# Four heads per update of x, context read back by batch, and the inner layer of batches 1 to 3 turned to [feature, token], in a two-block gated transformer kernel

## The chip, the cores and the metric

The kernel runs on one core of one Trainium2 chip. The metric is the device time of one execution in microseconds (us). The engines named below are PE (TensorE, matmuls), PEld (its weight loads), DVE (VectorE), ACT (ScalarE), POOL (GpSimd) and SP (the queue that issues most DMAs). PSUM is the memory that PE writes; it has eight banks here, each of 128 partitions x 512 float32.

## The reference

Four batches (b) of 512 tokens x 512 features pass through two blocks. Everything is float32 at the interface. Cut to what is computed:

```python
# block 0: adjacency from the context, top 153 of 512 per row, made symmetric
sim  = einsum(Q, K) / (sqrt(32) * 4);  keep = sim >= 153rd largest of its row
A    = sigmoid(sim) * keep;  A = (A + A.T) / 2
x    = x + tanh(g_x[0]) * ((1 - gamma) * layernorm(x) + gamma * A)
# block 0: feed-forward, Hadamard-rotated, 8-bit activations, ternary weights
h    = act_quant(fwht(layernorm(x)))          # fwht over 512
y    = silu(h @ gate.T) * (h @ up.T)          # 2048 features: the inner layer
x    = x + tanh(g_f[0]) * (act_quant(fwht(y)) @ down.T)   # fwht over 2048
# block 1: latent attention, 16 heads, keys and values from the context (kv, 128 wide, with rope)
q_r  = rope(layernorm(x) @ Wq @ w_kc_q) @ W_qr;  k_r = rope(kv) @ W_kr
x    = x + tanh(g_x[1]) * sum_h( softmax(q_r @ k_r.T) @ rope(kv) @ (w_kc_kv[h] @ Wo[h]) )
# block 1: feed-forward with rms norm, 8-bit activations, ternary weights
x    = x + tanh(g_f[1]) * (n + act_quant(silu(gate(n)) * value(n)) @ out.T)
```

## The kernel before

Each batch's 512 tokens are four tiles (j) of 128 tokens on the partitions, kept in SBUF as `xs[b, j]`. The program has three stages.

**Start.** Batch 0 goes alone through block 0 (`adjacency(0)`, `feed0(0, w0)`), while the weights of block 0's feed-forward are made ternary (`ternary`) and `ahead` prepares the attention: it multiplies the context by its rope tables on POOL (`kv[b]`, one tile for each batch that stays in SBUF for the whole kernel), and multiplies `w_kc_kv[h]` by `Wo[h]` into one 128 x 512 matrix for each head, which is stored to DRAM (`om_d[h]`).

**Attention with background work.** `attention` runs over 32 pairs of heads (4 batches x 8 pairs, class `Pair`). A pair has four steps j; each computes the scores of two heads, the softmax (DVE row maximum, ACT exp, DVE reciprocal, ACT scaling) and the transposes of the probabilities (`turn`); in between the next pair's queries are made (`head`, `rope`, `rotated`). Then `attended` multiplies by `kv` into `pc`, which ACT copies to `cxo`, and `added` multiplies by the two heads' `om` into PSUM (`po`, two products summed for each j) and DVE adds it to x (L870). The loads of `om` are issued by `out_weights` at the start of the pair.

Between the steps, generators of background work are advanced by estimated costs: `before(b)` (adjacency, keys and `feed0` of the next batch) during the attention of the batch before it, and `last_weights` (the ternary weights of block 1 and `feed1` of batches 0 to 2) during batch 3. In `feed0` of batches 1 to 3, `gated` multiplies the quantized tokens of a tile `zq` by the ternary weights `wa` (float8): for each of four groups o of 512 features, four matmuls make the gate in `pg`, four the up part in `pu`, with tokens on the partitions; ACT applies silu with the token's scale (L307), DVE multiplies (L308). `back` does the Hadamard transform over 2048 features: butterflies across the sixteen blocks of 128 features on DVE (L551), then, in four rounds, four PE transposes (`ph`, L557), a copy to SBUF on ACT (`yT`, L559), four matmuls with the 128 x 128 Hadamard matrix (`pzh`, L563) and a scaled copy on ACT (`yb`, L564). `projected` finds the row maximum, quantizes, transposes and multiplies by the down weights (`pd`, L399).

**End.** `feed1` of batch 3 and the rest of the background work.

A list scheduler orders every engine's instructions when the program is built, by priority (the order of the program, shifted in `high_priority` blocks) and by its own estimate of durations; on the chip each engine runs its list strictly in order. PSUM has four banks for the attention (`mm`), two for transposes (`tr`) and two for background work (`bg`): in the background `pg`, `pu`, `ph`, `pzh` and `pd` all take turns in the two `bg` banks. A float32 matmul is recorded as two PE records, a float32 transpose or a bfloat16 or float8 matmul as one.

Of the kernel before, what the change touches and what calls it, by code (L numbers as in the profile page):

```python
# [2 lines left out]

# [23 lines left out]
EPS = 1e-5  # L27
MAGIC = 12582912.0
GONE = -3.0e38
F8 = mybir.dt.float8e4  # L30


@with_exitstack
def flamingo_kernel(
# [51 lines left out]
    def front_t(name):  # L86
        if mine("front", 2):
            return two_k("front", 3, name)
        return wp.tile([P, 512], F32, tag="pp", name=name, bufs=7)

    def gate_t(name):
        if alone[0]:
# [122 lines left out]
    def ternary(specs, names, hold):  # L215


        found = []

        def piece(src, inner, i, name):  # L220
            t = big(f"{name}{i}")
            marks["load"] = nc.sync.dma_start(
                t if inner == 1 else t.rearrange("p (c o) -> p c o", c=inner), src(i)
            )
            return t

        for (src, inner, n, dst, count), name in zip(specs, names):
            acc = small.tile([P, n], F32, tag=f"wacc{n}", name=f"acc_{name}")
            held = []
            for i in range(n):  # L230
                t = piece(src, inner, i, f"sa_{name}")
                held.append(t)
                junk = bp.tile([P, FF], BF, tag="q", name=f"ja_{name}{i}") if hold else t
                nc.scalar.activation(junk, t, AF.Abs, accum_out=acc[:, i : i + 1])
                yield 4.0
            tot = small.tile([P, 1], F32, tag="wtot", name=f"tot_{name}")
            nc.vector.tensor_reduce(tot, acc, AX.X, ALU.add)
            pt = bg_ps(f"pt_{name}")
            marks["sum"] = nc.tensor.matmul(pt[:, 0:1], ones, tot, start=True, stop=True)
            sc = const.tile([P, 1], F32, tag=f"ws_{name}", name=f"ws_{name}")  # L240
            nc.vector.tensor_scalar(sc, pt[:, 0:1], 1.0 / count, EPS, ALU.mult, ALU.max)
            inv = const.tile([P, 1], F32, tag=f"wi_{name}", name=f"wi_{name}")
            nc.vector.reciprocal(inv, sc)
            found.append(sc)
            for i in range(n):
                t = held[i] if hold else piece(src, inner, i, f"sb_{name}")
                nc.scalar.activation(t, t, AF.Identity, scale=inv, bias=magic[:, 0:1])
                marks["sign"] = nc.scalar.activation(
                    dst(i), t, AF.Sign, bias=magic[:, 1:2], saturate=False
                )  # L250
                yield 4.0
        return found
# [42 lines left out]
    def gated(u, zq, wa, dg, y):  # L295

        for o in range(4):
# [10 lines left out]
            nc.vector.tensor_tensor(y[:, o * 512 : (o + 1) * 512], sg, pu, ALU.mult)  # L308
            yield 0.9

    reached = []

    def tiles(name, ready, wa, back, spread):
# [186 lines left out]
    def feed0(b, w):  # L500
# [44 lines left out]
        def back(j, ya, du):  # L545
            u = f"f{b}_{j}"
            yb = big(f"yb_{u}")

            for src, dst, g in ((ya, yb, 8), (yb, ya, 4), (ya, yb, 2), (yb, ya, 1)):
                for args in butterfly(src, dst, "p (g t q) -> p g t q", {"g": g}):  # L550
                    nc.vector.tensor_tensor(*args)  # L551
                    yield 1.3
            for k in range(4):
                pt = bg_tr(f"ph_{u}_{k}")
                for c in range(4):
                    at = (4 * k + c) * P
                    nc.tensor.transpose(pt[:, c, :], ya[:, at : at + P], ident)  # L557
                hT_ = back_t(f"yT_{u}_{k}")
                nc.scalar.copy(hT_, pt.rearrange("p c q -> p (c q)"))  # L559
                pz = bg_ps(f"pzh_{u}_{k}")  # L560
                for c in range(4):
                    cols = slice(c * P, (c + 1) * P)
                    nc.tensor.matmul(pz[:, cols], hT_[:, cols], had_sb, start=True, stop=True)  # L563
# [84 lines left out]

    NG = NH // 2
    kv, hT = {}, {}  # L650
    om_d, kr_d = {}, {}
    spilled = {}

    def ahead():
# [5 lines left out]
        sin_k = wp.tile([P, NT, DC], F32, tag="rs", name="sin_k", bufs=3)  # L660
        nc.gpsimd.dma_start(sin_k, sink)
        hf = DC // 2
        for b in range(B):
            cb = wp.tile([P, NT, DC], F32, tag="qh", name=f"cb_{b}")
            nc.gpsimd.dma_start(cb, cx[b * S : (b + 1) * S, :].rearrange("(j p) d -> p j d", p=P))
            t = const.tile([P, NT, DC], F32, tag=f"kv{b}", name=f"kv_{b}")
            nc.gpsimd.tensor_tensor(t, cb, cos_k, ALU.mult)
            rt = wp.tile([P, NT, DC], F32, tag="rs", name=f"rt_{b}", bufs=3)
            nc.gpsimd.tensor_tensor(rt[:, :, :hf], cb[:, :, hf:], sin_k[:, :, :hf], ALU.mult)
            nc.gpsimd.tensor_tensor(rt[:, :, hf:], cb[:, :, :hf], sin_k[:, :, hf:], ALU.mult)  # L670
            nc.gpsimd.tensor_tensor(t, t, rt, ALU.add)
            kv[b] = t
        yield
        for h in range(NH):
            wv = hp.tile([P, DC], F32, tag="wk", name=f"wv_{h}", bufs=3)
# [5 lines left out]
            om = wp.tile([P, D], F32, tag="cxo", name=f"oms_{h}", bufs=3)  # L681
# [6 lines left out]

    def keys(b):

        pt = bg_tr(f"pkv_{b}")
        for j in range(NT):
            nc.tensor.transpose(pt[:, j, :], kv[b][:, j, :], ident)
# [4 lines left out]
        for g in range(NG):  # L698
# [2 lines left out]
            pk = gate_ps(f"pk_{b}_{g}")  # L701
            nc.tensor.matmul(pk, wk, kvT, start=True, stop=True)
            if alone[0]:
                k = wp.tile([P, S], F32, tag="cxo", name=f"krs_{b}_{g}", bufs=3)
            else:
                k = front_t(f"krs_{b}_{g}")
            nc.scalar.copy(k, pk)
# [5 lines left out]
    def hidden_T(b):  # L713
        mv, r = ln_stats([xs[b, j] for j in range(NT)], f"q{b}")
        t = hp.tile([P, NC, S], F32, tag="hT", name=f"hT_{b}", bufs=1)
        for j in range(NT):
            n = wp.tile([P, D], F32, tag="pp", name=f"nq_{b}_{j}", bufs=7)
# [21 lines left out]
    def out_weights(b, g):  # L739

        oms = []
        for h in (2 * g, 2 * g + 1):
            om = hp.tile([P, D], F32, tag="om", name=f"om_{b}_{h}")
            nc.sync.dma_start(om, om_d[h])
            oms.append(om)
        return oms
# [7 lines left out]
    class Pair:  # L754
# [60 lines left out]
        def scores(self, j):  # L815
# [12 lines left out]
            for i in range(2):  # L828
                v = f"{self.u}_{i}_{j}"
                nm = small.tile([P, 1], F32, tag="nm", name=f"nm_{v}")  # L830
                nc.vector.tensor_reduce(nm, pss[i], AX.X, ALU.max, negate=True)  # L831
                pp = wp.tile([P, S], F32, tag="pp", name=f"pp_{v}", bufs=7)
# [15 lines left out]
        def attended(self):  # L848
            self.cxo = []
            for i in range(2):  # L850
                pc = mm_ps(f"pc_{self.u}_{i}")
                for l in range(NT):
# [4 lines left out]
                cxo = wp.tile([P, S], F32, tag="cxo", name=f"cxo_{self.u}_{i}", bufs=3)  # L857
                nc.scalar.copy(cxo, pc)  # L858
                self.cxo.append(cxo)

        def added(self):
            for j in range(NT):
                po = mm_ps(f"po_{self.u}_{j}")
                for i in range(2):
                    nc.tensor.matmul(  # L865
                        po, self.cxo[i][:, j * P : (j + 1) * P], self.oms[i],
                        start=(i == 0), stop=(i == 1),
                    )
                t = xs[self.b, j]
                nc.vector.scalar_tensor_tensor(t, po, tgx1, t, ALU.mult, ALU.add)  # L870
# [6 lines left out]
    def attention(first):  # L877
# [4 lines left out]
        for at, (b, g) in enumerate(order):  # L882
# [256 lines left out]
```

## Time and profile before

| | |
|---|---|
| median of 3 runs | 2063.09 us (2061.5 to 2064.79) |
| the profiled execution | 2064.35 us, span 2062.6 us |
| PE busy | 1853.7 us (90%), 7274 records |
| DVE busy | 1584.7 us (77%) |
| ACT busy | 1176.6 us (57%) |
| POOL busy | 333.1 us (16%) |
| DMA | 139.25 MB, mean 68 GB/s |
| mean granted TensorE clock | 0.962 |

The span divides into the start (to about 290 us), the attention with background work (to about 1970 us) and the end. Inside the attention, the gating of batches 1, 2 and 3 (L302) lies at 487 to 583, 904 to 1007 and 1321 to 1424 us, and block 1's weights are made ternary between 1451 and 1578 us. A busy PE is not PE at its peak, since the ends of matmul records are modelled; the distance from the start of one record to the start of the next is the better price of a matmul in a stream.

### The profile page before, as it was taken

The page shows a single profiled execution, that of the slowest core. Times are in us where ns is not written, and L with a number is a line of the kernel's source. Part 1 is how long each engine was busy: PE and PEld are TensorE (multiplying, and loading weights), DVE is VectorE, ACT ScalarE, POOL GpSimd, SP SyncE. Part 2 cuts the span into 40 slices and gives each one's busy share as a digit, 9 for nine tenths or more (in the row PEclk, how much of TensorE's full clock was granted, in tenths as well). Part 3 has the DMA queues.
Part 4 walks back from the last instruction along what each step waited for, and adds up shares of the span by engine and source line. Part 5 has one row for each costly group of instructions (what it writes and reads, how often), then busy time and mean ns, then how long its engine had stood idle before and what let it go on. Part 6 is the DMA issues. An engine that isn't in the chain of part 4 may idle for free. (4 is left out here: it accounts for less than half of the span.)

```text
span 2062.6 us, 21752 instructions
## 1 busy us (share of the span) xinstructions
PE 1853.7 (90%) x7274; PEld 873.3 (42%) x7274; DVE 1584.7 (77%) x3233; ACT 1176.6 (57%) x1979; POOL 333.1 (16%) x316
## 2 busy tenths in 40 slices
PE   1268789999999999999999999999999999999898
PEld 0035434434544444445453444454444444444344
DVE  7989599986774999876769999767636755866775
ACT  6935454455544555455454554554899565567554
POOL 3010031122100221230011221300112210101000
PEclk6579899999999999999999999999999999999999
DMA  7451021210101222110012221101755111111000
GB/s 273 148 177 38 1 77 41 63 46 27 38 21 32 83 82 60 43 38 26 27 33 87 72 73 38 38 21 33 256 191 199 50 38 45 58 35 39 11 16 26
DMA packets 65633, 139.25 MB, mean 68 GB/s; under 512 B 7537, under 2 KB 18161, under 8 KB 62449
## 3 DMA queue, kind: packets, MB, share of 16 engines
q1 hardware_dynamic: 60048, 121.92, 18.7%
q0 software_dynamic: 4320, 14.16, 1.8%
q10 hardware_dynamic: 1152, 1.77, 0.2%
q8 instruction: 58, 0.95, 0.2%
q14 instruction: 55, 0.44, 0.1%
HBM read 117.90 MB, written 19.92 MB: 67 GB/s over the span
## 5 line engine op out<-in xcount | busy, mean ns | idle before, releaser
L793 POOL TENSOR_TENSOR ro<-ro,rs 128x512 f32<-128x512 f32 x192 | 252.7, 1319 | 1167.2 <-DVE rs L789 753.8
L834 ACT ACTIVATE pp<-pss,nm 128x512 f32<-128x512 f32 x256 | 175.1, 688 | 224.8 <-DVE nm L831 224.0
L764 PE MATMUL pqh<-hT,wq 128*128 128x512 f32 x512 | 239.6, 603 | 6.8 <-ACT pp L834 6.6
L853 PE MATMUL pc<-pT,kv 128*128 128x512 f32 x512 | 235.4, 598 | 0.7 <-ACT pT L846 0.6
L865 PE MATMUL po<-om,cxo 128*128 128x512 f32 x512 | 230.9, 597 | 0.0
L831 DVE TENSOR_REDUCE nm<-pss 128x1 f32<-128x512 f32 x256 | 167.6, 681 | 57.4 <-PE pss L826 56.5
L779 PE MATMUL pb<-qh,wc 128*128 128x512 f32 x384 | 191.1, 614 | 10.4 <-ACT qh L769 7.3
L449 DVE MAX8 m<-work 128x8 f32<-128x512 f32 x304 | 198.0, 680 | 0.6
L454 DVE MATCH_REPLACE8 work<-m,work 128x512 f32<-128x512 f32 x288 | 192.8, 674 | 0.1
L837 ACT ACTIVATE pp<-pp,rsm 128x512 f32<-128x512 f32 x256 | 178.9, 724 | 21.2 <-DVE rsm L836 20.9
L870 DVE SCALAR_TENSOR_TENSOR x<-po,gt,x 128x512 f32<-128x512 f32 x128 | 94.6, 744 | 92.4 <-PE po L865 91.9
L846 ACT COPY pT<-ppt 128x512 f32<-128x512 f32 x256 | 142.9, 592 | 28.9 <-PE ppt L845 28.8
L845 PEld LDWEIGHTS ppt<-ident,pp 128*128 128x128 f32 x1024 | 117.3, 141 | 86.0 <-issue 33.9
L845 PE MATMUL ppt<-ident,pp 128*128 128x128 f32 x1024 | 146.4, 277 | 6.7 <-ACT pT L846 3.5
L823 PE MATMUL pss<-kr,qr 64*128 64x512 f32 x256 | 144.3, 644 | 5.6 <-ACT pp L834 4.8
L764 PEld LDWEIGHTS pqh<-hT,wq 128*128 128x128 f32 x512 | 92.7, 191 | 125.4 <-issue 84.6
L826 PE MATMUL pss<-kr,qr 64*128 64x512 f32 x256 | 144.4, 645 | 0.5 <-DVE ro L787 0.5
L865 PEld LDWEIGHTS po<-om,cxo 128*128 128x128 f32 x512 | 93.7, 190 | 114.5 <-issue 98.1
L787 DVE TENSOR_TENSOR ro<-pb,cos_q 128x512 f32<-128x512 f32 x192 | 130.5, 680 | 11.0 <-PE pb L779 10.2
L853 PEld LDWEIGHTS pc<-pT,kv 128*128 128x128 f32 x512 | 92.7, 190 | 102.3 <-issue 88.7
L858 ACT COPY cxo<-pc 128x512 f32<-128x512 f32 x64 | 37.6, 587 | 135.7 <-PE pc L853 135.4
L750 PE MATMUL pr<-ro,wr 128*64 128x512 f32 x192 | 99.8, 613 | 14.3 <-POOL ro L793 12.2
(266 smaller groups left out, 3123.5 us busy)
## 6 DMA issues: line engine op xcount, KB each, us to landing
wq<-in_wqh SPq DMA_DIRECT2D x64, 256.0 KB, 2.7
om<-omd SPq DMA_DIRECT2D x64, 256.0 KB, 2.7
wc<-in_wkcq SPq DMA_DIRECT2D x32, 384.0 KB, 3.1
krd<-krs POOLq DMA_DIRECT2D x32, 256.0 KB, 2.4
kr<-krd SPq DMA_DIRECT2D x32, 256.0 KB, 2.7
sa_w1v<-in_gvT SPq DMA_DIRECT2D x8, 1024.0 KB, 5.3
sb_w1v<-in_gvT SPq DMA_DIRECT2D x8, 1024.0 KB, 5.5
wr<-in_wqr SPq DMA_DIRECT2D x32, 192.0 KB, 2.4
```

The costliest lines, as they stand in the source:

```text
L449: nc.vector.max(m8[j], cur[j])
L454: nc.vector.match_replace(works[j], m8[j], cur[j], GONE)
L764: nc.tensor.matmul(pq, self.wqs[i][:, c, :], hT[self.b][:, c, :], start=(c == 0), stop=(c == NC - 1),)
L779: nc.tensor.matmul(pb, self.wc[:, at : at + P], self.qhs[i if i < 2 else o], start=True, stop=True)
L793: nc.gpsimd.tensor_tensor(ro, ro, rs, ALU.add)
L826: nc.tensor.matmul(*args, start=True, stop=True)
L831: nc.vector.tensor_reduce(nm, pss[i], AX.X, ALU.max, negate=True)
L834: nc.scalar.activation(pp, pss[i], AF.Exp, bias=nm, accum_out=sm)
L837: nc.scalar.activation(pp, pp, AF.Copy, scale=rs)
L845: nc.tensor.transpose(pt[:, l, :], pp[:, l * P : (l + 1) * P], ident)
L853: nc.tensor.matmul(pc, kv[self.b][:, l, :], self.pT[i][:, l, :], start=(l == 0), stop=(l == NT - 1),)
L865: nc.tensor.matmul(po, self.cxo[i][:, j * P : (j + 1) * P], self.oms[i], start=(i == 0), stop=(i == 1),)
```

## The change

**x updated for four heads at once.** `added` runs for every second pair only and takes the `cxo` and `om` of both pairs: four products are summed in PSUM for each j, and DVE adds the sum to x. `cxo` gets four buffers (from three), `om` four (from two); `pp`, the tile of probabilities, gets six (from seven).

**Context read back by batch.** `ahead` goes through the batches from 3 down to 0; the rope'd contexts of batches 3, 2 and 1 are stored to DRAM on POOL's queue, and `keys(b)` reads them back on SP's. `kv` now has two buffers in place of four tiles.

**Inner layer of batches 1 to 3 as [feature, token].** `gated_turned` takes the weights as the stationary operand and the tokens as the moving one, 128 columns at a time, so that y has features on the partitions, block by block. Each token's scale then lies along the free axis: it is spread over a 128 x 128 row tile (DVE, one PE product with the identity, ACT copy), DVE multiplies `pg` by it, and ACT applies silu in SBUF. The four transposes and the copy of each round in `back` are gone: `pzh` reads y.

**One step of the ternary weights of block 1 on DVE.** Where the weights are not held (`hold` false), the scaling with the rounding constant moves from ACT to DVE.

```diff
     def front_t(name):
-        return wp.tile([P, 512], F32, tag="pp", name=name, bufs=7)
+        return wp.tile([P, 512], F32, tag="pp", name=name, bufs=6)
...
                 t = held[i] if hold else piece(src, inner, i, f"sb_{name}")
-                nc.scalar.activation(t, t, AF.Identity, scale=inv, bias=magic[:, 0:1])
+                if not hold:
+                    nc.vector.tensor_scalar(t, t, inv, MAGIC, ALU.mult, ALU.add)
+                else:
+                    nc.scalar.activation(t, t, AF.Identity, scale=inv, bias=magic[:, 0:1])
...
+    def gated_turned(u, zq, wa, dg, y):
+        row = front_t(f"dgr_{u}")
+        nc.vector.tensor_scalar(row[:, :P], ones, dg, None, ALU.mult)
+        pt = bg_ps(f"pdg_{u}")
+        nc.tensor.matmul(pt[:, :P], row[:, :P], ident, start=True, stop=True)
+        nc.scalar.copy(row[:, P : 2 * P], pt[:, :P])
+        row = row[:, P : 2 * P].unsqueeze(1).to_broadcast([P, 4, P])
+        for o in range(4):
+            pg = gate_ps(f"pg_{u}_{o}")
+            pu = gate_ps(f"pu_{u}_{o}")
+            for pw, at in ((pg, FF + o * 512), (pu, o * 512)):
+                for f in range(4):
+                    cols = slice(at + f * P, at + (f + 1) * P)
+                    for c in range(NC):
+                        nc.tensor.matmul(
+                            pw[:, f * P : (f + 1) * P], wa[:, c, cols], zq[:, c, :],
+                            start=(c == 0), stop=(c == NC - 1),
+                        )
+            sg = gate_t(f"sg_{u}_{o}")
+            nc.vector.tensor_tensor(
+                sg.rearrange("p (f t) -> p f t", f=4), pg.rearrange("p (f t) -> p f t", f=4), row, ALU.mult
+            )
+            nc.scalar.activation(sg, sg, AF.Silu)
+            nc.vector.tensor_tensor(y[:, o * 512 : (o + 1) * 512], sg, pu, ALU.mult)
+            yield 0.9
...
-            return gated(f"{name}_{j}", zq, wa, dg, y), back(j, y, du)
+            made = gated_turned if spread and not alone[0] else gated
+            return made(f"{name}_{j}", zq, wa, dg, y), back(j, y, du)
...
-                pt = bg_tr(f"ph_{u}_{k}")
-                for c in range(4):
-                    at = (4 * k + c) * P
-                    nc.tensor.transpose(pt[:, c, :], ya[:, at : at + P], ident)
-                hT_ = back_t(f"yT_{u}_{k}")
-                nc.scalar.copy(hT_, pt.rearrange("p c q -> p (c q)"))
+                if quick:
...
+                else:
+                    hT_ = ya[:, 4 * k * P : 4 * (k + 1) * P]
...
-        for b in range(B):
+        for b in reversed(range(B)):
...
-            kv[b] = t
+            if b == 0:
+                kv[b] = t
+            else:
+                kv_d[b] = dram.tile([P, NT, DC], F32, tag=f"kvd{b}", name=f"kvd_{b}")
+                nc.gpsimd.dma_start(kv_d[b], t)
...
     def keys(b):
+        if b:
+            kv[b] = wp.tile([P, NT, DC], F32, tag="kv", name=f"kvr_{b}")
+            nc.sync.dma_start(kv[b], kv_d[b])
...
-        def added(self):
+        def added(self, before):
+            cxo, oms = before.cxo + self.cxo, before.oms + self.oms
             for j in range(NT):
                 po = mm_ps(f"po_{self.u}_{j}")
-                for i in range(2):
+                for i in range(4):
                     nc.tensor.matmul(
-                        po, self.cxo[i][:, j * P : (j + 1) * P], self.oms[i],
-                        start=(i == 0), stop=(i == 1),
+                        po, cxo[i][:, j * P : (j + 1) * P], oms[i], start=(i == 0), stop=(i == 3)
                     )
...
-            cur.added()
+            if g % 2:
+                cur.added(last)
+            last = cur
```

More of the change, by code (lines that the diff above doesn't have):

```diff
@@ L1 @@
 import math
-from contextlib import ExitStack
+from contextlib import ExitStack, nullcontext
 import concourse.bass as bass
@@ L29 @@
 GONE = -3.0e38
+U16 = mybir.dt.uint16
 F8 = mybir.dt.float8e4
@@ L553, in back @@
             for k in range(4):
-                pt = bg_tr(f"ph_{u}_{k}")
-                for c in range(4):
-                    at = (4 * k + c) * P
-                    nc.tensor.transpose(pt[:, c, :], ya[:, at : at + P], ident)
-                hT_ = back_t(f"yT_{u}_{k}")
-                nc.scalar.copy(hT_, pt.rearrange("p c q -> p (c q)"))
+                if quick:
+                    pt = bg_tr(f"ph_{u}_{k}")
+                    for c in range(4):
+                        at = (4 * k + c) * P
+                        nc.tensor.transpose(pt[:, c, :], ya[:, at : at + P], ident)
+                    hT_ = back_t(f"yT_{u}_{k}")
+                    nc.scalar.copy(hT_, pt.rearrange("p c q -> p (c q)"))
+                else:
+                    hT_ = ya[:, 4 * k * P : 4 * (k + 1) * P]
                 pz = bg_ps(f"pzh_{u}_{k}")
@@ L650, in flamingo_kernel @@
     kv, hT = {}, {}
-    om_d, kr_d = {}, {}
+    om_d, kr_d, kv_d = {}, {}, {}
     spilled = {}
@@ L662, in ahead @@
         hf = DC // 2
-        for b in range(B):
+        for b in reversed(range(B)):
             cb = wp.tile([P, NT, DC], F32, tag="qh", name=f"cb_{b}")
             nc.gpsimd.dma_start(cb, cx[b * S : (b + 1) * S, :].rearrange("(j p) d -> p j d", p=P))
-            t = const.tile([P, NT, DC], F32, tag=f"kv{b}", name=f"kv_{b}")
+            t = wp.tile([P, NT, DC], F32, tag="kv", name=f"kv_{b}")
             nc.gpsimd.tensor_tensor(t, cb, cos_k, ALU.mult)
@@ L680, in ahead @@
             nc.tensor.matmul(po, wv, wo, start=True, stop=True)
-            om = wp.tile([P, D], F32, tag="cxo", name=f"oms_{h}", bufs=3)
+            om = wp.tile([P, D], F32, tag="cxo", name=f"oms_{h}", bufs=4)
             nc.scalar.copy(om, po)
@@ L703, in keys @@
             if alone[0]:
-                k = wp.tile([P, S], F32, tag="cxo", name=f"krs_{b}_{g}", bufs=3)
+                k = wp.tile([P, S], F32, tag="cxo", name=f"krs_{b}_{g}", bufs=4)
             else:
@@ L716, in hidden_T @@
         for j in range(NT):
-            n = wp.tile([P, D], F32, tag="pp", name=f"nq_{b}_{j}", bufs=7)
+            n = wp.tile([P, D], F32, tag="pp", name=f"nq_{b}_{j}", bufs=6)
             ln_tile(n, xs[b, j], j, mv, r)
@@ L742, in out_weights @@
         for h in (2 * g, 2 * g + 1):
-            om = hp.tile([P, D], F32, tag="om", name=f"om_{b}_{h}")
+            om = hp.tile([P, D], F32, tag="om", name=f"om_{b}_{h}", bufs=4)
             nc.sync.dma_start(om, om_d[h])
@@ L831, in scores @@
                 nc.vector.tensor_reduce(nm, pss[i], AX.X, ALU.max, negate=True)
-                pp = wp.tile([P, S], F32, tag="pp", name=f"pp_{v}", bufs=7)
+                pp = wp.tile([P, S], F32, tag="pp", name=f"pp_{v}", bufs=6)
                 sm = small.tile([P, 1], F32, tag="sm", name=f"sm_{v}")
@@ L856, in attended @@
                     )
-                cxo = wp.tile([P, S], F32, tag="cxo", name=f"cxo_{self.u}_{i}", bufs=3)
+                cxo = wp.tile([P, S], F32, tag="cxo", name=f"cxo_{self.u}_{i}", bufs=4)
                 nc.scalar.copy(cxo, pc)
                 self.cxo.append(cxo)
-        def added(self):
+        def added(self, before):
+            cxo, oms = before.cxo + self.cxo, before.oms + self.oms
             for j in range(NT):
                 po = mm_ps(f"po_{self.u}_{j}")
-                for i in range(2):
+                for i in range(4):
                     nc.tensor.matmul(
-                        po, self.cxo[i][:, j * P : (j + 1) * P], self.oms[i],
-                        start=(i == 0), stop=(i == 1),
+                        po, cxo[i][:, j * P : (j + 1) * P], oms[i], start=(i == 0), stop=(i == 3)
                     )
```

## The prediction

> **What bounds the kernel now.** I read the page's busy times and its forty slices first, then the windows of the stages that the change touches, then the timelines of the gating and of the Hadamard rounds, then the waits of single tiles.
>
> ```profile
> PE 1853.7 (90%) x7274; PEld 873.3 (42%) x7274; DVE 1584.7 (77%) x3233; ACT 1176.6 (57%) x1979; POOL 333.1 (16%) x316
> ...
> PE   1268789999999999999999999999999999999898
> ...
> PEclk6579899999999999999999999999999999999999
> ```
>
> From slice 5 on PE is at nine tenths in nearly every slice. Busy is modelled, so I price a record by the distance from its start to the next start in a stream: 0.430 us for a float32 record of 512 columns, 0.216 for a float8 one (below), 0.110 for a float32 one of 128. Priced so, PE's records between 440 and 1450 us fill 87 to 90% of the time. PE is the bound, and some 12% of the time goes in short gaps, so an instruction removed from PE counts nearly in full, and one removed from DVE or ACT only through a gap on PE.
>
> ```profile
> 440.00:670.00 230.00, 221.05 (x952) 110.81 (x950) 156.55 (x269) 115.97 (x213) 35.07 (x34) 0.98 0.10 30
> 860.00:1090.00 230.00, 223.01 (x965) 111.66 (x964) 158.66 (x277) 117.88 (x219) 37.34 (x34) 1.00 0.10 31
> 1275.00:1450.00 175.00, 170.29 (x740) 84.32 (x737) 125.13 (x215) 88.72 (x161) 30.60 (x30) 1.00 0.11 33
> 1450.00:1590.00 140.00, 129.68 (x462) 60.91 (x461) 73.70 (x151) 131.13 (x175) 22.07 (x17) 0.98 0.68 230
> ```
>
> The windows (columns: busy PE, PEld, DVE, ACT, POOL, then clock and DMA) show the three stretches with feed0's gating, where DVE is at 70% and ACT at 50%, and the making of block 1's ternary weights (the last line), where ACT is at 94%. Two timelines of PE, the first at the gating of batch 1, the second at the Hadamard rounds of batch 3:
>
> ```profile
> 491.65 1.03 PE L302 MATMUL pu_f<-wa_w,zq_f 128*128 128x512 fp8e4 x4
> 492.59 1.02 PE L302 MATMUL pg_f<-wa_w,zq_f 128*128 128x512 fp8e4 x4
> 493.53 1.02 PE L302 MATMUL pu_f<-wa_w,zq_f 128*128 128x512 fp8e4 x4
> 494.39 1.02 PE L302 MATMUL pg_f<-wa_w,zq_f 128*128 128x512 fp8e4 x4
> 495.40 1.02 PE L302 MATMUL pu_f<-wa_w,zq_f 128*128 128x512 fp8e4 x4
> ```
> ```profile
> 1343.08 0.60 PE L557 MATMUL ph_f<-ident,ya_f 128*128 128x128 f32 x4
> 1343.52 1.02 PE L853 MATMUL pc<-pT,kv 128*128 128x512 f32 x2
> 1344.38 1.14 PE L563 MATMUL pzh_f<-had_sb,yT_f 128*128 128x128 f32 x8
> 1345.35 0.60 PE L557 MATMUL ph_f<-ident,ya_f 128*128 128x128 f32 x4
> ```
>
> The gating runs almost without gaps: 1.87 us for each group o, of which 8 x 0.216 = 1.73 are matmuls. A Hadamard round costs 0.44 of transposes, and its `pzh` comes one foreign matmul later, because the copy `yT` lies between.
>
> ```profile
> 1360.90 0.62 PE L202 MATMUL ptq_hf<-identb,q_f 128*128 128x128 bf16 x8 [0.29 <-DVE q_f L210]
> 1361.36 1.08 PE L764 MATMUL pqh<-hT,wq 128*128 128x512 f32 x2
> 1362.27 0.61 PE L202 MATMUL ptq_hf<-identb,q_f 128*128 128x128 bf16 x8
> 1362.72 1.94 PE L764 MATMUL pqh<-hT,wq 128*128 128x512 f32 x4
> ```
>
> This is the row nearest to the new matmuls: a 16-bit weight load and 128 columns, eight in 0.45 us, 0.056 each.
>
> **The change part by part.** The sum is made on the profiled execution, 2064.35 us (span 2062.6 and 1.75 around it), which is 1.26 above the median of 2063.09.
>
> *Turned matmuls.* Twelve tiles lose 32 records of 512 columns and get 128 of 128 columns. Before: 384 x 0.216 = 83.0 us (pd_f, the same kind, has 16 in 3.46). After: 1536 x 0.056 = 86.0, +3.1. No row has float8 as the stationary operand. The lower bound is the column rate, 0.216/4 = 0.054, +0; the upper is a weight load that is not hidden, 0.098 (mean of the 16-bit load of L302), 150.5 us, +67.6. I take 0.056: same columns, and an element no wider.
>
> *A page against it.* The Trainium skill, "TensorE: Matmul & The Clock Gate", section "Back-to-back issue gap", gives about 81 ns for each pair of load and matmul at 128 columns in a sustained stream; the row above shows 56. By the page the term would be +41.4, and the whole sum +28 in place of -10.
>
> *Transposes.* 12 x 16 `ph` at 0.110 = 21.1 us go from PE. The scale's row tile adds 12 x 2 records at 0.12 = +2.9. PE alone: 3.1 - 21.1 + 2.9 = -15.1.
>
> *Hadamard rounds.* In the timeline a round takes 2.27 to 2.32 us, of which 0.44 + 0.86 + 8 x 0.111 = 2.19 is work; 48 rounds at 0.13 lost make -6. Bounds: 0 (the gap only moves to other records) and -15 (0.3 a round, the mean of the gaps in front of the first `pzh` records over the starts of all 48 rounds); I take the timeline's value, since some of a gap moves on. What is late next is ACT's `yb`, 0.60 for each `pzh` of 0.89 in two banks: covered.
>
> *The gate's chain.* Here a wait is added. Before, `pu` of the next group waits for ya of this one (DVE 0.69, ACT's silu beside the matmuls). After, `pg` goes through DVE (0.68), ACT (0.69) and DVE (0.68) with about 0.2 between them, before the next `pu` finds its bank: 2.55 us for a group against 1.8 of matmuls, 0.75 open. Queued behind a waiting `pu` is all of PE. The changed kernel's order of PE puts other work into these loops: of the 36 loops inside tiles, 24 get 0.75 us or more (a `pqh`, `pb`, `pc` or `po` product at 0.87, or `ppt` and `pr`), and the rest leave 5 us open in all. But in the second tile of each batch DVE's order has butterflies of 1.23 between the new multiplies: 3.8 us of DVE in a loop with 2.0 to 3.1 of PE, some 2.5 a tile, 7.5. Rope and row-maximum instructions in front of the multiplies I put at 2. Sum +14; bounds 0 (all filled) and 48 x 0.75 + 7.5 = +43.
>
> *Other DVE and ACT work.* DVE: +48 multiplies x 0.68, +12 x 0.2, +12 scalings of 128 x 2048 at 1.3 (L382 has 1.28 to 1.37), -64 sums at 0.744 (L870): +33 + 2 + 16 - 48 = +3. ACT: -48 `yT` at 0.587, -12 scalings at 2.09 (L247), +12 small copies at 0.3: -50. In the ternary window PE's gaps are 18% against 12% in the stretches around 1100 to 1270, an excess of 8 us, with ACT at 94%; there ACT loses 25 us and DVE, at 53%, gets 16. I take -4 (0 to -8). Elsewhere neither bounds: 0.
>
> *Four heads at once.* PE's `po` records stay as many. Between the last `po` and the next scores PE loses 0.09 us in every pair now, so the halved DVE sums free nothing there: 0. On even pairs the scores follow `pc` directly; `cxo`, which they do not need, is copied beside them. SP's waits for `om` (422.6 us, SP L744 <- PE po) shrink, but no PE wait hangs on them. Six `pp` hold the three live steps of two heads; only the four tiles of `hidden_T` at three batch changes are tighter, +1 (0 to +4).
>
> *Context read back.* Three stores on POOL's queue (0.56 each to issue) and three loads on SP's. The first load stands in SP's order before the block-0 weight piece that went out at 39.7 us; the rope work on POOL ended at 30.7 before, and with the store landed I expect the load by 35: hidden. If it comes after, it delays ACT's ternary chain, which ends at 102 while the gating that reads it begins at 146. The other two wait for `pc` of the last pair, as x's stores beside them wait for `po`; keys use them tens of us later. 0 (up to +2).
>
> Sum: -15.1 - 6 + 14 - 4 + 1 = -10, so 2054 for such an execution and **2053** for the median.
>
> **Rivals.** A measurement of this kernel tells about 0.2% (4.1 us) from no change, so 2059 to 2067 is "same".
>
> *R1, the turned pairs run slower than 0.056* (the other side). The place is the 128 matmuls of a tile, the price 1536 times the excess. At 0.063 the gain is gone, at 0.070 it is 11 us slower than before, at 0.098 2117. For it: no row has a float8 weight load, and the streams I see end after 16 pairs. Against: all such streams at full clock run at 0.055 to 0.057.
>
> *R2, the gate's chain is not covered.* With 34 to 43 in place of 14 the sum is +10 to +19: 2073 to 2082; at 24 it decides against the gain. For it: DVE is at 70% there and strictly in order. Against: 24 of 36 loops have their filler.
>
> *R3, everything is covered and the relief of ACT is real*: chain +2, rounds -12, ternary -8: about 2031.
>
> **How the numbers follow.** My case, 2040 to 2059: 0.42. R3, 2027 to 2040: 0.12. R2, 2059 to 2082: 0.27, of which 0.10 lies below 2067. R1, 2067 to 2117: 0.19. Faster 0.42 + 0.12 = 0.54, same 0.10, slower 0.17 + 0.19 = 0.36. The range leaves out the slower half of R1 and the fast end of R3: 2031 to 2092. My case alone has 2040 to 2059.
>
> **What would show it.** Right: turned records 0.056 apart; no `ph` and no `yT` after 290 us; four `pzh` in a row in about 3.6 us; gating of the first two tiles of batch 1 in 20 to 23 us (18.1 before); `added`'s DVE sums 64 in place of 128; ACT under 80% in the ternary window. Wrong: records 0.07 or more apart (R1); PE waits before `pu` of 1 us and more in most loops (R2); a half-speed clock in the gating; or a start that ends later than before, with SP held by the context's load.

## The result, and the profile after

The changed kernel takes 2067.97 us (median of 20 runs, 2064.21 to 2074.36), the kernel before beside it 2064.67 (20 runs): a ratio of 1.0018, 95% interval 1.0010 to 1.0026. It is slower by 3.7 us where I had forecast 10 us less, so the direction was wrong, though the time lies in the range. The profiled execution took 2067.19 us, with a span of 2065.3.

The changed kernel's page, busy times and slices of PE and of its granted clock:

```profile
PE 1848.8 (90%) x8258; PEld 910.0 (44%) x8258; DVE 1587.9 (77%) x3241; ACT 1125.9 (55%) x1927; POOL 337.5 (16%) x319
...
PE   1268799999999999999999999999889999999898
...
PEclk6579899999999999999999999999999999999899
```

Its windows, with the bounds of those shown of before (busy PE, PEld, DVE, ACT, POOL, then clock, DMA share, GB/s):

```profile
440.00:670.00 230.00, 219.01 (x1297) 122.17 (x1295) 171.51 (x304) 114.78 (x214) 39.55 (x37) 1.00 0.11 31
860.00:1090.00 230.00, 221.43 (x1312) 123.52 (x1311) 169.85 (x304) 116.49 (x221) 43.54 (x39) 1.00 0.12 34
1275.00:1450.00 175.00, 170.44 (x1099) 99.35 (x1098) 133.95 (x230) 86.87 (x160) 31.24 (x31) 0.99 0.16 50
1450.00:1590.00 140.00, 123.50 (x418) 56.23 (x417) 88.06 (x188) 106.61 (x160) 26.29 (x18) 0.95 0.61 208
```

And its PE timeline at the gating of batch 1 and at a tile's Hadamard rounds:

```profile
494.40 1.05 PE L331 MATMUL pg_f<-zq_f,wa_w 128*128 128x128 bf16 x16
495.29 1.06 PE L331 MATMUL pu_f<-zq_f,wa_w 128*128 128x128 bf16 x16
496.30 1.05 PE L331 MATMUL pg_f<-zq_f,wa_w 128*128 128x128 bf16 x16
...
510.08 3.79 PE L599 MATMUL pzh_f<-had_sb,ya_f 128*128 128x128 f32 x32
```

What was counted came as counted. Sixteen turned records take 0.89 us, 0.056 each; four `pzh` rounds run on end; ACT has lost 51 us, DVE has gained 3. In the first fence PE even has less to do. But in the last window, the ternary one, PE is busy 6 us less in the same 140 us at a lower clock: idle time has been added.

**A finer ruler.** ACT's copy `qr` ends the making of a pair's queries, one for each of 32 pairs. I cut every profiled execution at the `qr` of every fourth pair. Where two kernels give a stretch the same instructions in the same order, its length mostly repeats to 0.3 us, rarely 0.6 (the changed kernel and e4, whose PE, DVE and ACT have the same order after the start, agree so from S1 to S7; S8 differs by 2.1. In e7 and e16, also of one order, S5 differs by 1.5), while the start wanders by several. So a stretch shows what the totals, with some 8 us between the lowest and the highest run of a kernel, can't. In the table T is the turned layer, K the context read back, H the four-head sums with their buffers, D the ternary step on DVE. S1, S3, S5, S7 are pairs 0 to 3 of a batch (the top-k of the next batch, in S7 block 1's weights), S2, S4, S6 are pairs 4 to 7 with the gating of batches 1, 2 and 3, and S8 is batch 3's last four pairs and the end. With H a block of products of 7 us passes from S1 to S8; this is no change in time. The last column is the time after the start for which the clock rows of the same profile show half clock.

```
kernel (parts)                   start     S1     S2     S3     S4     S5     S6     S7     S8   half
before                           284.5  149.6  255.3  169.5  247.2  169.6  250.1  183.3  353.4   28.6
changed (T K H D)                288.6  142.6  247.3  170.9  243.3  171.0  252.7  184.3  364.5   47.8
e1 (T)                           288.2  149.7  250.3  169.7  246.6  169.7  253.8  183.3  354.9   35.2
e2 (D)                           285.3  149.7  255.3  169.5  247.2  169.6  254.1  182.7  353.6   35.4
e6 (K)                           289.0  149.7  255.4  169.8  247.7  169.8  252.6  184.0  352.0   31.2
e3 (K H)                         287.7  142.6  260.8  168.3  245.5  171.4  256.0  184.6  364.1   58.0
e13 (T K)                        286.8  149.7  250.3  169.7  243.1  170.3  250.9  183.7  352.8   27.9
e5 (T K H)                       291.1  142.6  247.3  171.0  243.3  171.0  251.6  183.1  364.0   41.4
e8 (T without its multiply)      283.6  149.7  247.5  169.7  241.8  170.3  244.7  183.3  355.8   20.5
e14 (changed, without it)        289.6  142.7  246.7  171.0  241.3  171.0  251.0  180.0  363.6   41.4
e11 (changed, idle DVE work)     287.8  142.5  254.8  168.0  243.4  169.4  250.9  179.8  365.0   41.4
e7 (changed, H spread)           287.1  142.4  243.5  172.1  243.9  171.8  252.1  181.4  363.1   55.0
e16 (e7, batch 1 kept)           289.7  142.4  243.5  171.8  244.0  170.3  250.5  180.9  362.7   47.8
e9 (e16, step on ACT)            289.6  142.4  243.5  170.3  242.3  171.8  249.6  190.6  363.3   55.1
e4 (changed, batch 1 kept)       290.9  142.6  247.3  171.2  243.4  171.0  252.8  183.7  362.4   41.7
e10 (e3, H spread)               288.7  142.4  247.3  171.8  250.6  172.2  256.6  183.8  362.8   55.1
e12 (e9, rounding on ACT)        288.3  142.4  248.0  170.5  245.4  171.8  249.8  189.8  359.9   48.6
e15 (before, six pp)             285.4  149.7  255.3  169.7  247.2  169.9  249.7  184.1  352.7   28.6
```

### The profile page after: what moved, and what is told of

Same layout as the page of the kernel before. It is cut to its first block, busy times and chain, and to the rows that moved or that the text cites. A ratio compares the mean times of both kernels' runs of the same rounds, so it can differ in the third digit from the quotient of the medians.

```text
span 2065.3 us, 23630 instructions
## 1 busy us (share of the span) xinstructions
PE 1848.8 (90%) x8258; PEld 910.0 (44%) x8258; DVE 1587.9 (77%) x3241; ACT 1125.9 (55%) x1927; POOL 337.5 (16%) x319
## 5 line engine op out<-in xcount | busy, mean ns | idle before, releaser
L910 PE MATMUL po<-om,cxo 128*128 128x512 f32 x512 | 224.7, 593 | 0.0
L822 PE MATMUL pb<-qh,wc 128*128 128x512 f32 x384 | 192.0, 617 | 13.6 <-ACT qh L812 7.4
L896 PE MATMUL pc<-pT,kvr 128*128 128x512 f32 x384 | 178.3, 601 | 0.2 <-ACT pT L889 0.2
L888 PE MATMUL ppt<-ident,pp 128*128 128x128 f32 x1024 | 151.5, 283 | 9.0 <-ACT pp L880 4.3
L822 PEld LDWEIGHTS pb<-qh,wc 128*128 128x128 f32 x384 | 65.9, 191 | 103.8 <-issue 37.8
L331 PEld LDWEIGHTS <-wa_w 128*128 128x128 fp8e4 x1536 | 89.8, 98 | 32.3 <-issue 29.8
```

The costliest lines, as they stand in the source:

```text
L822: nc.tensor.matmul(pb, self.wc[:, at : at + P], self.qhs[i if i < 2 else o], start=True, stop=True)
L888: nc.tensor.transpose(pt[:, l, :], pp[:, l * P : (l + 1) * P], ident)
L896: nc.tensor.matmul(pc, kv[self.b][:, l, :], self.pT[i][:, l, :], start=(l == 0), stop=(l == NT - 1),)
L910: nc.tensor.matmul(po, cxo[i][:, j * P : (j + 1) * P], oms[i], start=(i == 0), stop=(i == 3))
```

## The experiments

Ratios are to the kernel before on the same chip, with 95% intervals; times in us are the ratio's distance from 1 by 2064. A difference between two of these kernels is uncertain by 2 to 3 us.

**One part at a time.** `e1_turned` turns only the inner layer of the kernel before; beside this choice it has `gated_turned` and the shorter `back` of the change:

```diff
-            return gated(f"{name}_{j}", zq, wa, dg, y), back(j, y, du)
+            made = gated_turned if spread and not alone[0] else gated
+            return made(f"{name}_{j}", zq, wa, dg, y), back(j, y, du)
```

> The kernel before with only the inner layer of batches 1 to 3 turned; seven pp buffers, sums for two heads, the context in SBUF, the ternary step on ACT. Theory A (each part of the change acts for itself, and the turned part is a gain that the other parts give away): PE loses 15 us of work, the Hadamard rounds lose 9 us of gaps and the gate's chain adds 6, so 12 to 18 us under before, about 2050, with the start and the ternary window at the times of before. Theory B (the gain of the turned part is eaten inside the gating, by DVE in order): within 3 us of before, 2062 to 2067.

Measured: 2064.25, ratio 0.9996 (0.9985 to 1.0007): -0.8 us, theory B. In S2 it gains 5.0, in S4 0.6, in S6 it loses 3.7. The groups of PE, and then the window, of e1 between the ends of pairs 11 and 15, which hold the gating of batch 2:

```profile
L877 PE MATMUL ppt<-ident,pp 128*128 128x128 f32 x128 | 18.8, 278 | 1.6 <-ACT pp L869 1.1 <-ACT hT L754 0.3 <-ACT pT L878 0.2
L327 PE MATMUL pg_f<-zq_f,wa_w 128*128 128x128 bf16 x256 | 16.9, 219 | 1.0 <-DVE sg_f L332 1.0
```
```profile
875.00:1117.80 242.80, 232.28 (x1343) 128.54 (x1342) 186.92 (x334) 119.61 (x226) 43.22 (x36) 1.00 0.12 35
```

The same two views of the kernel before, between the same two marks:

```profile
L845 PE MATMUL ppt<-ident,pp 128*128 128x128 f32 x128 | 18.2, 276 | 0.3 <-ACT hT L722 0.3
L302 PE MATMUL pg_f<-wa_w,zq_f 128*128 128x512 fp8e4 x64 | 16.4, 379 | 0.1
```
```profile
876.00:1119.50 243.50, 237.17 (x1016) 117.69 (x1014) 176.35 (x314) 126.93 (x238) 42.15 (x36) 1.00 0.12 34
```

PE lost 5 us of work, DVE gained 10.6, and the stretch of 243 us became 0.7 shorter: PE now waits for the new multiplies (`sg`) and for the softmax (`pp`): these two rows hold 2.2 us of the 4.2 by which PE's idle time grew here. That the softmax is late because DVE's list is fuller is likely, but not isolated.

`e2_ternary`:

```diff
+                if not hold:
+                    nc.vector.tensor_scalar(t, t, inv, MAGIC, ALU.mult, ALU.add)
+                else:
                     nc.scalar.activation(t, t, AF.Identity, scale=inv, bias=magic[:, 0:1])
```

> The kernel before with only the first ternary step of block 1's weights on DVE. Theory A (DVE, in order, is held by the load of a weight piece, and the attention's steps behind it wait): +2 to +5 us over before, about 2068, with waits of DVE for the piece's load. Theory B (the prediction's step: ACT's relief counts): -4 (0 to -8), about 2061.

Measured: 2067.72, 1.0009 (0.9999 to 1.0018): +1.9, nearer to theory A, though the interval still reaches no change; the stretches that change are S6 (+4.0), where the making of the weights begins, and S7 (-0.6). DVE's timeline in the changed kernel shows a wait of the kind that theory A had, and below it PE at the same time:

```profile
1483.95 1.28 DVE L249 TENSOR_SCALAR sb_w1v<-sb_w1v,wi_w1v 128x2048 f32<-128x2048 f32 x1
1490.30 1.29 DVE L249 TENSOR_SCALAR sb_w1v<-sb_w1v,wi_w1v 128x2048 f32<-128x2048 f32 x1 [5.07 <-DMA sb_w1v<-in_gvT]
```
```profile
1485.69 1.11 PE L764 MATMUL phT<-ident,nq 128*128 128x128 f32 x4 [1.26 <-ACT hT L765]
1488.55 5.37 PE L807 MATMUL pqh<-hT,wq 128*128 128x512 f32 x8 [0.89 <-ACT hT L765]
```

The second instruction waits 5.07 us for its piece of the weights, and DVE, which is in order, waits with it, and so do the row maxima and rope behind it. With the step on ACT (before, e5) no wait of ACT for these pieces is recorded. But PE, meanwhile, waits for ACT's copies `hT`, as it does in e5 with the step on ACT (1.35 and 0.89 us). And e16 below has a DVE wait of 5.73 us at the same place and is the faster for having the step on DVE. So the wait is shown, but not that it is what the step costs.

`e3_heads_context` takes the four-head sums, `pp` six, `cxo` four, `om` four and the read-back from the change, `e6_context` the read-back alone (with the stores, the reversed order of the batches and two `kv` buffers):

```diff
+        if b:
+            kv[b] = wp.tile([P, NT, DC], F32, tag="kv", name=f"kvr_{b}")
+            nc.sync.dma_start(kv[b], kv_d[b])
```

> The kernel before with only the sums for four heads and the context read back by batch (with their buffers: pp six, cxo four, om four, kv two). Theory A: +4 to +5 at the start, where SP holds the weight pieces behind the context's load, and about +2 for each of three top-k stretches, with pairs of uneven length: +8 to +11 in all, about 2074. Theory B (the prediction's steps: both free): 0 to +1, about 2065, and the lengthening seen in the changed kernel comes from the other parts.

> The kernel before with only the context read back by batch (two kv buffers); x is updated for two heads, pp, cxo and om have their old buffers. It divides the +18 us of the run with four heads and the context together. Theory A (the four-head sums and their buffers are the cause): 0 to +4, at the start, so 2065 to 2069. Theory B (the read-back and its place in SP's and POOL's queues is the cause): +12 to +18, 2077 to 2083.

Measured: e3 2083.17, 1.0087 (1.0071 to 1.0102), +18, beyond theory A; e6 2068.99, 1.0023 (1.0014 to 1.0031), +4.7, nearer to A. So H with its buffers costs 13 us alone, and not in the top-k stretches, where theory A had put it: against K alone it adds 5.4 in S2, 3.4 in S6 and, the 7 us apart, 5 in S8. `e15_pp6` is the kernel before with six `pp`:

> The kernel before with six pp buffers in place of seven (for the probabilities, for the front's tiles and for the four tiles of hidden_T), nothing else. Theory A (the buffers are what the four-head part costs alone): +8 to +13, 2073 to 2078. Theory B (the prediction's +1, 0 to +4): 2064 to 2068.

Measured: 2066.44, 1.0012 (1.0004 to 1.0021), +2.5: theory B; these buffers are a small part, and its profile does not place even that (S1 to S8 add up to those of before within 0.5). The larger `cxo` and `om` were not tested by themselves.

**The start.** SP's waits in the changed kernel show the read-back held for its own store, ahead of the weight pieces. Below the wait are the read-back and the next weight pieces in SP's timeline:

```profile
SPq L733 <- DMA kvd<-kv: 9.9, 1, 9.9
```
```profile
34.73 0.33 SPq L733 DMA_DIRECT2D kvr<-kvd  x1
42.05 8.08 SPq L223 DMA_DIRECT2D sa_w0u<-in_upT  x3
```

`e4_keep_kv1` takes this load away:

```diff
-        for b in reversed(range(B)):
+        for b in (3, 2, 0, 1):
...
-            if b == 0:
+            if b < 2:
                 kv[b] = t
```

> The changed kernel, but the context of batch 1 is kept in its SBUF tile from the start on, so that its store and its load on SP's queue are gone; batches 2 and 3 are read back as in the change, and the orders of DVE and ACT are those of the changed kernel. Theory A (that load holds the weight pieces behind it, and so the whole start): queries of the first pair 4 us earlier, the end 3 to 5 us earlier, about 2064. Theory B (the start's delay is from something else, or is caught up later): within 1 us of the changed kernel, 2067 to 2069.

Measured: 2067.21, 1.0007 (0.9997 to 1.0017), 2.3 us under the changed kernel, between the theories, but its start is not shorter (290.9). Over all profiles the start takes 283.6 to 288.2 us in five kernels without the read-back (mean 285.4) and 286.8 to 291.1 in thirteen with it (mean 288.8), 289.6 in the four of these that keep batch 1. So K costs 3.4 at the start, in the mean, but not through this load: it is issued 7 us before the next weight piece, which waits 6.9 us for ACT (`wa_w`), and in e4, without the load, that piece goes out at 42.11. ACT itself is late by then: it ends the gate's first weights at 49.3 to 50.5 us in the five kernels and at 51.2 to 52.8 in the thirteen. Through which part of K (stores, order of the batches, buffers) stays open.

**Parts beside each other.** +18 and -0.8 and +1.9 do not make +3.7. `e5_ternary_act` is the changed kernel with D undone; `e13_turned_context` is T and K without H and D.

> The changed kernel with the ternary step of block 1's weights back on ACT (the other three parts as changed). Theory A (the step costs where DVE is in order, +1.9 us alone on the kernel before): 2 to 4 us under the changed kernel, 2064 to 2066. Theory B (the prediction's step, ACT's relief is worth 4 us, and shows once the other parts are there): 4 us over the changed kernel, about 2072.

> The kernel before with the turned inner layer and the context read back; sums for two heads, the ternary step on ACT, pp seven buffers. To be set against the same with four-head sums (no difference from before, 1.0000). Theory A (the four-head sums gain beside the turned layer): the two parts add, -0.8 and +4.7, so about 4 us over before, 2067 to 2070. Theory B (the four-head sums cost their 13 us in any company): 8 to 13 us under before, 2051 to 2056.

Measured: e5 2066.74, 1.0000 (0.9991 to 1.0010): D costs 3.7 here, theory A. e13 2059.13, **0.9978** (0.9969 to 0.9986): neither expectation. The read-back, +4.7 alone, is -3.7 beside T, and H on top of both costs 4.5. Of that, S8 has 4.1 (the 7 us apart). The windows around pair 31 of e13 and of e5, which differ by H alone:

```profile
1905.00:1915.00 10.00, 9.35 (x25) 3.58 (x24) 8.65 (x22) 2.67 (x5) 0.00 (x0) 1.00 0.17 52
1915.00:1925.00 10.00, 6.27 (x37) 3.50 (x38) 10.00 (x34) 9.03 (x20) 0.00 (x0) 1.00 0.00 1
1925.00:1935.00 10.00, 6.84 (x29) 2.93 (x30) 2.59 (x7) 9.91 (x17) 0.00 (x0) 0.83 0.00 0
```
```profile
1905.00:1915.00 10.00, 8.98 (x23) 3.16 (x21) 8.41 (x28) 4.50 (x10) 0.00 (x0) 0.96 0.00 1
1915.00:1925.00 10.00, 8.83 (x28) 4.70 (x28) 8.48 (x28) 6.60 (x14) 0.00 (x0) 0.50 0.01 2
1925.00:1935.00 10.00, 7.22 (x29) 4.45 (x30) 4.82 (x16) 9.62 (x19) 0.00 (x0) 0.51 0.00 0
```

With H the clock falls to half for 20 us, without it for 3 us. The same event, 17 to 20 us long at 1906 to 1931, is in every profile with H and in none without (there the longest at this place is 6.8).

**Why the turned layer gained nothing alone.** `e8_no_scale` is e1 without the multiply by the scale's row, `e14_no_scale_all` the changed kernel without it; both leave the scaling of the gate out of what they compute:

```diff
-            nc.vector.tensor_tensor(
-                sg.rearrange("p (f t) -> p f t", f=4), pg.rearrange("p (f t) -> p f t", f=4), row, ALU.mult
-            )
-            nc.scalar.activation(sg, sg, AF.Silu)
+            nc.scalar.activation(sg, pg, AF.Silu)
```

> The kernel before with the turned inner layer alone, and without the multiply by the tokens' scales: silu reads pg as it is (the row of scales is still made). This leaves the scaling of the gate out of the computation and takes 48 DVE instructions of 0.68 us, some 33 us, and a link of the gate's chain away. Theory A (the turned part's gain is eaten by DVE, which is in order and gets these multiplies): 10 to 15 us under before, 2050 to 2055. Theory B (removed PE work turns into idle time for another reason, the softmax chain of the attention): within 4 us of before, 2061 to 2067.

> The changed kernel without the multiply by the tokens' scales in the turned layer (the scaling of the gate is left out of the computation, and 48 DVE instructions, 33 us, with it); all other parts as changed. On the kernel before with the turned layer alone the same took 16 us away. Theory A (the halved sums have already made room on DVE for these multiplies): only 0 to 6 us under the changed kernel, 2062 to 2068. Theory B (the multiplies cost the same wherever they stand, as a link of the gate's chain): 12 to 17 us under it, 2051 to 2056.

Measured: e8 2048.03, 0.9917 (0.9903 to 0.9931), -17, theory A and more; so the 48 multiplies, DVE's work and the link in the gate's chain together, cost 16 us in e1, all in S2, S4 and S6 (16.7). e14 2059.3, 0.9976 (0.9966 to 0.9986): they cost 8.7 in the changed kernel, between the theories.

If H makes room for them on DVE, filling that room must cost. `e11_dve_back` does so, in the even pairs:

```diff
+            else:
+                for j in range(NT):
+                    idle = small.tile([P, 1], F32, tag="nm", name=f"idle_{b}_{g}_{j}")
+                    nc.vector.tensor_reduce(idle, xs[b, j], AX.X, ALU.max)
```

> The changed kernel with DVE's load put back: for each even pair four row maxima of x into an unused 128 x 1 tile, where the two-head sums stood, 64 DVE instructions of about 0.68 us, some 44 us of DVE, which nothing reads. Theory A (DVE is a second bound, and the turned layer gains only because the four-head sums give DVE back what its multiplies take): 10 to 18 us over the changed kernel, 2078 to 2086. Theory B (DVE has slack beside PE, as the prediction had it): 0 to 3 us over it, 2068 to 2071.

The added instructions are all there (duration in ns, minimum, median and maximum):

```profile
L957 DVE TENSOR_REDUCE idle<-x x64: 655/677/689, 311.5 to 1894.6; 128x1 f32<-128x512 f32 x64
```

Measured: 2063.47, 0.9999 (0.9990 to 1.0008), 3.9 us *under* the changed kernel. Theory A falls as a sum over the kernel. By stretches it holds in one place: S2 is 7.5 longer (6.8 us of it at half clock, worth 3.4 at most); S3, S5, S6 and S7 are 1.6 to 4.5 shorter, with more work. The added instructions change the planner's picture of DVE and so the orders after it: PE's differs from its 307th record after the start on.

**Spreading the four-head products.** `e7_spread` is the changed kernel with `added` called for one j in each step of the next pair; `e10_heads_spread` does it to e3:

```diff
+                if late:
+                    late[0].added(late[1], [j])
                 if j > 1:
                     cur.turn(j - 2)
...
-            if g % 2:
-                cur.added(last)
+            late = None
+            if g == NG - 1:
+                cur.added(last)
+            elif g % 2:
+                late = cur, last
```

> The changed kernel, but the four-head products of x are not made in one block after the odd pair: each of the four tiles gets its four products in one step j of the next pair (the last pair of a batch keeps its block). Same instructions, same counts. Theory A (a block of 32 po records, 14 us of PE, makes DVE wait in the top-k stretches, where DVE is busy 84.05 of 86.30 us in the kernel before and 82.05 of 89.50 in the changed one): those stretches go back by 2 to 3 us each and the even pairs too, in all 5 to 10 us under the changed kernel, 2058 to 2063. Theory B (the block is harmless, the loss is from the buffers or from the read-back): 2066 to 2070.

> The kernel before with the four-head sums spread over the steps of the next pair and the context read back, nothing else; to be set against the run with the block of four-head sums, 18 us over before, and the context alone, 5 us over it. Theory A (the block of 32 po records is what the four heads cost): 0 to 6 us over before, 2065 to 2071. Theory B (the cost is in the buffers, pp six above all, or in om's loads): 12 to 18 us over before, 2077 to 2083.

The reason for trying it is in DVE's timeline of the changed kernel at the end of a block (top-k has just ended there):

```profile
448.35 0.75 DVE L914 SCALAR_TENSOR_TENSOR x<-po,gt,x 128x512 f32<-128x512 f32 x1 [0.95 <-PE po L910]
451.78 0.75 DVE L914 SCALAR_TENSOR_TENSOR x<-po,gt,x 128x512 f32<-128x512 f32 x1 [1.22 <-PE po L910]
454.18 0.55 DVE L184 TENSOR_SCALAR n_f<-x,mv_f,r_f 128x512 f32<-128x512 f32 x1 [1.64 <-PE pn_f L555]
```

Measured: e7 2058.70, **0.9971** (0.9960 to 0.9982), 9.7 under the changed kernel, the size that theory A gave, but not its place: S2 gains 3.8 and S7 2.9, S3 and S5, the top-k stretches, are 0.8 to 1.2 longer. e10 2077.8, 1.0067 (1.0054 to 1.0081): without T the spread saves only 4 of 18, theory B there: it saves 13.5 in S2 and loses 9.4 in S3 to S5.

**Joining the gains.** `e9_joined` is T, K and H with the spread, batch 1 kept and the ternary step on ACT; `e12_round_act` adds the removal of the rounding constant (`q`, 24 instructions, nearly all of 1.2 us on DVE and 2.0 on ACT) on ACT; `e16_spread_keep` is e7 with batch 1 kept, the step on DVE.

> The turned inner layer and the four-head sums, these spread over the steps of the next pair, with the ternary step back on ACT and the context of batch 1 kept in SBUF (batches 2 and 3 read back). Theory A (the gains found one by one add up: 6 us under before from the spread, about 2 from the ternary step, 0 to 2 from the kept context): 8 to 11 us under before, 2054 to 2057. Theory B (they share the same idle time): 2057 to 2060.

> As the run that joins the gains, and the removal of the rounding constant from the quantized inner layer (128 x 2048 to bfloat16, 24 times 1.3 to 1.4 us on DVE in the attention stage) goes to ACT. Theory A (DVE's time counts, ACT's does not): 2 to 6 us under the joined run. Theory B (the long ACT instruction holds the softmax's exponentials, in order, and gives it back): 0 to 4 us over it.

> The changed kernel with the four-head sums spread over the next pair's steps and the context of batch 1 kept in SBUF; the ternary step stays on DVE. Theory A (beside spread sums the ternary step on DVE is a gain): 0 to 4 us under the run with the sums spread alone, 2055 to 2059, with the stretch of batch 3's first four pairs at about 181 us, as there. Theory B (that run's advantage over the joined one was from the stored and reloaded context): 2061 to 2064, with that stretch at about 190 us.

Measured: e9 2062.84, 0.9990 (0.9981 to 0.9999), worse than either theory; e12 2068.58, 1.0025 (1.0014 to 1.0036): theory B's side and beyond it, relieving DVE costs 7; e16 2057.69, **0.9964** (0.9950 to 0.9978), theory A and the lowest median of the kernels that compute everything, though not clear of e7. Between e9 and e16 the ternary step alone differs: on DVE it gains 5.4, in S7 9.7 (190.6 against 180.9; 10.2 us of S7 are at half clock in e9 and 1.4 in e16, worth 4.4 of the difference at most). The same edit loses 3.7 where the sums stand in a block.

## Why the prediction was wrong

*Taken in the order T, K, H, D, each on top of the others*, the parts give -0.8, -3.7, +4.5, +3.7; I had -7, 0, +1, -4. T is 6 short, H 3.5, and D, the largest miss, is off by 7.7 with the wrong sign; K hides 3.7 of it.

*Turned matmuls and transposes.* Right: 0.056 apart, R1 excluded. Summing all PE records at their start-to-start prices gives 1677 us before and 1662 after, -15 as forecast. The Trainium skill, "TensorE: Matmul & The Clock Gate", section "Back-to-back issue gap", has 81 ns for such a pair in a stream; streams of 16 turned pairs with a float8 weight load measure 55 to 56. What failed is the sentence that "an instruction removed from PE counts nearly in full". By the same pricing the time that no PE record fills went from 374 us to 392: it took the whole gain. After the start the growth is 14.5 us, and 13.6 of it lie at half clock: 14.4 us became 28.0, while at full clock 212.0 became 212.9 (e4, with the same orders: 24.1 and 214.4). (At half clock this time holds both idling and the slower records.) In e1, with T alone, it is the other way round: 14.4 became 18.2, but 212.0 became 223.9, so there T's gain goes to plain waits.

*Hadamard rounds.* -6 forecast; the gaps in front of the `pzh` records of the twelve tiles went from some 15 to 6.5 us, a little more than forecast. But in e1, with the same `back`, they stay at some 15, so this gain is not the layer's alone.

*The gate's chain.* +14 forecast, bounds 0 and 43. Its size is borne out: the multiply costs 16 us in e1 and 8.7 in the changed kernel. Its mechanism is so only in part. I had looked for the wait in front of `pu`, and by the same pricing the gaps before all turned records grew only from some 5 us to some 10; in e1 waits for softmax and rope stand beside them. e8 takes the link of the chain and DVE's work away at once, so the two are not told apart. R2 as worded, PE waiting 1 us and more before most `pu`, did not happen.

*The ternary step on DVE.* -4 (0 to -8) forecast, +3.7 measured, outside the bounds. I saw ACT at 94% and DVE at 53% and took the queue for a bound by load. Busy shares say nothing of what a waiting instruction blocks, and the 5.07 us for which DVE waits for a piece were not in my sum. Why the step costs 3.7 here stays open all the same: PE does not stand still for that wait, and e16 gains with a longer one. ACT did fall under 80% in this window, as I had said, and PE's busy time fell as well.

*Four heads at once.* 0 forecast, and +1 for six `pp`; +4.5 measured beside T and K, +13 without T. The +1 was of the right size (+2.5, inside its bounds). The 0 rested on PE losing nothing between the last `po` and the next scores, which is true and not the point: even pairs lost 7 us of PE work and odd ones gained it, so pairs that were 40 to 46 us long where top-k runs now alternate (36.2, then 51.4, in batch 1's), and the last pair meets the half clock shown above. Against K alone (e6 to e3) the time that no PE record fills after the start grows at half clock from 16.7 us to 33.9 and falls at full clock from 212.4 to 207.8: what H costs stands there. Rhythm and clock are terms I did not have; no run tests either by itself.

*Context read back.* 0 (up to +2) forecast; +4.7 alone and -3.7 beside T. "I expect the load by 35: hidden" held: it went out at 34.7, and SP's 9.9 us held no weight piece up. The alarm I had named, a later start with SP held by the load, sounded, but taking the load away did not bring the start back. The term that failed is the 0 for the rest of K: the start is 3.4 later, and beside T the stretches gain.

*What stays open.* Why H costs 13 us on the kernel before and 4.5 beside T, and why K changes its sign. The stretches say where (S2 and S6, and S8 for H; S4 and S6 for K beside T). Room on DVE explains a part at most (e14: 16 becomes 8.7), since e11 and e12 both go against it. Except for the kept context (e4, e16) and six `pp` (e15), every edit makes the planner order the engines anew after the start, and S2 alone ranges from 243.5 to 260.8 us over kernels whose priced PE work in it differs by 7 at most (215.5 to 222.1). I take this for a common cause of the differences that no step explains; no run isolates it. A rival is in the same profiles: the granted clock. S2 takes 255.3 or 255.4 us in the four kernels with 10.2 us of it at half clock, 248.0 to 250.3 in the three with 3.4, and 243.5 to 247.5 in those with none; half clock is worth 5 of these 12 at most. It cannot be all: e7 has 55 us at half clock after the start, more than the changed kernel, and is 9.7 faster. Whether an order brings the half clock about, or the half clock stretches the order, is shown in one place only: in e7 and e16, which have one order after the start, S5 takes 171.8 us with 3.4 at half clock and 170.3 with none. There the clock differs by itself, and its price is 1.5.

## What to carry to other kernels

When engines run planned lists in order and the bound engine is only 85 to 90% filled, a few microseconds of work taken from it are a bid, not a gain: price what the edit does to the other lists, and doubt a sum whose largest terms differ in sign. Compare executions by stretches between fixed marks of the same work, which repeat here to 0.3 us, rarely 0.6, where the clock is the same, read the granted clock in each of them, and test each part both alone and beside the others, for its sign can change. If a sum is batched to save one engine's instructions, try to spread the batch over the following steps instead of leaving it in one block: here that saved 9.7 us beside T and 4 without it.

## What the runs showed of the hardware

The start took 283.6 to 288.2 us in five kernels that have the same order there, while the 149.6 us that follow repeat to 0.1. The granted clock fell to half where no gap between PE records was long: in the 10 us before the fall at 1915 in the changed kernel the longest was 0.85 us. (The Trainium skill, "TensorE: Matmul & The Clock Gate", section "What's actually happening", gives an idle window of about 3.4 us as the condition; no gap of that length is recorded here.) With one and the same order after the start, the changed kernel and e4 were at half clock for 47.8 and 41.7 us there, e7 and e16 for 55.0 and 47.8; in S5 of the latter two, 3.4 us of half clock cost 1.5. A kernel with sixty-four more DVE instructions that nothing reads, 41 us of them, was 4 us faster; the orders of its engines differ too.
